# Degrees, h W1 and the order of the attention layer: three rearrangements of a four-layer graph kernel on one core

## The chip, the cores and the metric

The kernel runs on one NeuronCore of a Trainium2 chip. The time is device microseconds (us) of that core. TensorE (PE) multiplies matrices, VectorE (DVE), ScalarE (ACT) and GpSimd (POOL) work on elements, and the DMA queues bring the 4096 x 4096 adjacency matrix from memory again and again. Nearly everything is fp32; behind layer 0 only the targets' terms go through TensorE in bf16.

## The reference

Four graph layers, each added to its input and layer-normalised. N = 4096 nodes, F = 128 features.

```python
x = layernorm(x + L0(x, adj))   # masked attention with two scalars per node (not touched by the change)
x = layernorm(x + L1(x, adj))   # twice: T0 W0 + T1 W1 + T2 W2, T1 = adj T0, T2 = 2 adj T1 - T0, then elu
x = layernorm(x + L2(x, adj))   # 4 heads: tau = adj^T * exp(max(.2 C, C)); z = (adj^T * tau / sum tau) @ h'
x = layernorm(x + L3(x, adj))   # h W_self + (adj h / deg) W_neigh, deg = max(sum of a row of adj, 1)
```

L1 needs four products with adj. L2 needs, for each head, the elementwise tau (summed by a matmul into `den`) and tau * adj (multiplied with the head's features into `num`). L3 needs one product with adj and the row sums `deg`.

## The kernel before

The stages follow each other in time: layer 0 until about 345 us, four products of the Chebyshev layer (345 to 1425 us), the attention layer in eight passes (four column windows `mp` of 1024 targets, two pairs of heads `hp`), of which the first runs beside the fourth product, and the end. The last layer's product runs in "pieces" (one matmul each) between the steps of the attention passes.

The degrees come from DVE additions beside the first product and eight short PE passes per block; h W1 is multiplied after the transposition of the third product's block:

```python
def degree(a, first_one):                       # called for each of the 64 chunks of the first product
    s = l1h.tile([P, 2, IB], F32, name="dhalf")
    nc.vector.tensor_add(s, a[:, 0:2, :], a[:, 2:4, :])
    ...                                         # two more additions of 512 columns into dsum
for ib, blk, p in propagate(lambda jt: x[:, jt, :], finished, degree):
    nc.scalar.copy(t1T[:, blk], p)
    for k in range(TB):
        nc.tensor.matmul(pd[:, k:k + 1], dsum[:, k * P:(k + 1) * P], ones, start=True, stop=True)
    ...
for ib, blk, p in propagate(lambda jt: v[:, jt, :]):        # third product
    ...
    for k in range(TB):
        nc.tensor.matmul(q[:, k, :], lvT[:, k * P:(k + 1) * P], ident, start=True, stop=False)
        for hh in range(HH):
            nc.tensor.matmul(q[:, k, :], hT[:, hh, ...], W1B[:, HH + hh, :], start=False, stop=hh == HH - 1)
```

A pass of the attention, 32 steps of 128 source nodes; the scheduler was free to reorder it:

```python
for nt in range(NT):
    ...                                                     # a: 128 x 1024 of adj; sq = a[:, 0:OWN]^2 by ScalarE
    for h in range(2):
        nc.vector.scalar_tensor_tensor(tau[:, h, :], D[h], E(h), a, op0=ALU.max, op1=ALU.mult)
    nc.vector.scalar_tensor_tensor(tau2[:, 0, 0:OWN], D[0][:, 0:OWN], E(0), sq, op0=ALU.max, op1=ALU.mult)
    nc.gpsimd.tensor_tensor(tau2[:, 0, OWN:WB], tau[:, 0, OWN:WB], a[:, OWN:WB], ALU.mult)
    nc.gpsimd.tensor_tensor(tau2[:, 1, :], tau[:, 1, :], a, ALU.mult)
    product(den, nt, tau, True)                             # four matmuls in four column groups
    late.append((nt, tau2))
    if len(late) > 1:
        product(num, *late.pop(0), False)
    yield                                                   # here one piece of the last layer's product
...                                                         # copies, transposes, z = num / den, all in one lump
```

`D[h]` is the term of the targets of head h, which TensorE writes into PSUM (`d`) at the start of a pass, and `E(h)` that of the sources. `OWN` is 704. After the second pass of a window, `layer3_block` normalises two blocks of 512 nodes and multiplies them with the last weights, also in one lump.

Of the kernel before, what the change touches and what calls it, by code (L numbers as in the profile page):

```python
# [32 lines left out]
def adj_resnorm_d4(ctx: ExitStack, tc: tile.TileContext, x_in, xT_in, adj, adjT, w0g, w0gT, a0, w1a, b1a,  # L33
# [54 lines left out]
    cs = const.tile([P, NT, H], F32, name="cs")  # L88
    flag = const.tile([1, 1], I32, name="flag")
# [19 lines left out]
    def normalize(r, g, on_act=False):  # L109

        tb = slice(g * TB, (g + 1) * TB)
        s = small.tile([P, TB], F32, name="rstd")
        nc.vector.tensor_scalar_add(s, mv[:, tb, 1], LN_EPS)
        nc.scalar.activation(s, s, AF.Sqrt)
        nc.vector.reciprocal(s, s)
        if on_act:
            m = small.tile([P, TB], F32, name="mean")
            nc.vector.scalar_tensor_tensor(m, mv[:, tb, 0], -1.0, s, op0=ALU.mult, op1=ALU.mult)
        for k in range(TB):
            if on_act:  # L120
                nc.scalar.activation(r[:, k, :], r[:, k, :], AF.Identity, bias=m[:, k:k + 1], scale=s[:, k:k + 1])
            else:
                nc.vector.tensor_scalar(r[:, k, :], r[:, k, :], mv[:, g * TB + k, 0:1], s[:, k:k + 1],
                                        op0=ALU.subtract, op1=ALU.mult)
# [322 lines left out]
    def network(usual):  # L447

        with ExitStack() as whole:
# [4 lines left out]
            with ExitStack() as first, ExitStack() as l1h_pool:  # L454
# [6 lines left out]
                if usual:  # L461
                    finished = layer0(ld, ps_acc, ps_tr, ps_mm)
                dv = state.tile([96, N], BF16, name="dv")
# [17 lines left out]
                def propagate(stationary, order=range(NB), look=None):  # L481


                    for ib in range(NB):
                        p = ps_acc.tile([P, IB], F32, name="pacc")
                        for n, c in enumerate(order):
                            a = chunk(ld, adjT, ib, c)
                            if look:
                                look(a, n == 0)
                            for k in range(TB):  # L490
                                nc.tensor.matmul(p, stationary(c * TB + k), a[:, k, :], start=n == 0 and k == 0,  # L491
                                                 stop=n == NB - 1 and k == TB - 1)
                        yield ib, slice(ib * IB, (ib + 1) * IB), p
# [8 lines left out]
                dsum = l1h.tile([P, IB], F32, name="dsum")  # L502

                def degree(a, first_one):

                    s = l1h.tile([P, 2, IB], F32, name="dhalf")
                    nc.vector.tensor_add(s, a[:, 0:2, :], a[:, 2:4, :])
                    if first_one:
                        nc.vector.tensor_add(dsum, s[:, 0, :], s[:, 1, :])
                    else:  # L510
                        nc.vector.tensor_add(dsum, dsum, s[:, 0, :])
                        nc.vector.tensor_add(dsum, dsum, s[:, 1, :])


                for ib, blk, p in propagate(lambda jt: x[:, jt, :], finished, degree):
                    nc.scalar.copy(t1T[:, blk], p)
                    pd = ps_mm.tile([P, TB], F32, name="pmm")
                    for k in range(TB):
                        nc.tensor.matmul(pd[:, k:k + 1], dsum[:, k * P:(k + 1) * P], ones, start=True, stop=True)
                    nc.vector.tensor_scalar_max(rdeg[:, ib * TB:(ib + 1) * TB], pd, 1.0)  # L520
                    q = transpose4(ps_tr, "ptr", lambda k: t1T[:, (ib * TB + k) * P:(ib * TB + k + 1) * P])
                    nc.vector.tensor_copy(t1[:, ib * TB:(ib + 1) * TB, :], q)
                nc.vector.reciprocal(rdeg, rdeg)
# [20 lines left out]
                for ib, blk, p in propagate(lambda jt: v[:, jt, :]):  # L544
                    lvT = l1w.tile([P, IB], F32, name="t2T")
                    nc.scalar.copy(lvT, p)
                    q = ps_tr.tile([P, TB, F], F32, name="ptr")
                    for k in range(TB):
                        nc.tensor.matmul(q[:, k, :], lvT[:, k * P:(k + 1) * P], ident, start=True, stop=False)
                        for hh in range(HH):  # L550
                            nc.tensor.matmul(q[:, k, :], hT[:, hh, (ib * TB + k) * P:(ib * TB + k + 1) * P],  # L551
                                             W1B[:, HH + hh, :], start=False, stop=hh == HH - 1)
# [73 lines left out]
            def attention(l2w, bufs, mp, hp):  # L626


                D = []
                for h in range(2):  # L630
                    d = ps_d.tile([P, 2, IB], F32, name=f"d{h}")
                    for mb in range(2):
                        nc.tensor.matmul(d[:, mb, :], selD[:, 2 * hp + h, :],
                                         dv[:, mp * WB + mb * IB:mp * WB + (mb + 1) * IB], start=True, stop=True)
                    D.append(d.rearrange("p b i -> p (b i)"))
                num = ps_nd.tile([P, IB], F32, name="num")
                den = ps_nd.tile([P, IB], F32, name="den")

                def product(acc, nt, r, is_den):
                    for h in range(2):  # L640
                        for mb in range(2):
                            q = 32 * (2 * h + mb)
                            nc.tensor.matmul(acc[q:q + 32, :], weights(nt, 2 * hp + h, is_den),  # L643
                                             r[:, h, mb * IB:(mb + 1) * IB], start=nt == 0, stop=nt == NT - 1)

                late = []
                for nt in range(NT):
                    if nt % 2 == 0:
                        a2t = ld.tile([P, 2, WB], F32, name="chunk")
                        nc.sync.dma_start(a2t, adj[mp, nt // 2])  # L650
                    a = a2t[:, nt % 2, :]
                    sq = l2w.tile([P, OWN], F32, name="sq", bufs=2)
                    nc.scalar.activation(sq, a[:, 0:OWN], AF.Square)  # L653
                    tau = l2w.tile([P, 2, WB], F32, name="tau", bufs=bufs)
                    tau2 = l2w.tile([P, 2, WB], F32, name="tau2", bufs=bufs)
                    E = lambda h: es[:, nt, 2 * hp + h:2 * hp + h + 1]
                    for h in range(2):
                        nc.vector.scalar_tensor_tensor(tau[:, h, :], D[h], E(h), a, op0=ALU.max, op1=ALU.mult)  # L658
                    nc.vector.scalar_tensor_tensor(tau2[:, 0, 0:OWN], D[0][:, 0:OWN], E(0), sq,  # L659
                                                   op0=ALU.max, op1=ALU.mult)  # L660
                    nc.gpsimd.tensor_tensor(tau2[:, 0, OWN:WB], tau[:, 0, OWN:WB], a[:, OWN:WB], ALU.mult)  # L661
                    nc.gpsimd.tensor_tensor(tau2[:, 1, :], tau[:, 1, :], a, ALU.mult)  # L662
                    product(den, nt, tau, True)
                    late.append((nt, tau2))
                    if len(late) > 1:
                        product(num, *late.pop(0), False)
                    yield
                product(num, *late.pop(0), False)
                nd = l2w.tile([P, 2, IB], F32, name="nd")
                nc.scalar.copy(nd[:, 1, :], den)  # L670
                nc.scalar.copy(nd[:, 0, :], num)
# [145 lines left out]
```

## Time and profile before

| | before |
|---|---|
| time, median of the first three runs | 2348.3 us (2347.94 to 2351.55) |
| profiled span | 2345.0 us |
| start of the fourth product | 1110.2 us |
| fourth product and first pass, until the copy of `den` | 347.1 us |
| seven further passes, from copy of `den` to copy of `den` | 800.4 us |
| from the last copy of `den` to the end | 87.2 us |

The last four rows divide the span of the profile and add up to it: they are taken from the timeline, the first from TensorE's first matmul with `w`, the borders of the passes from ScalarE's copies `nd<-den`. The question in each part is which engine's work sets the distance between two such marks. The views that answer it are shown in the prediction; one more is the list of what VectorE waited for in the seven passes (columns: instruction that waited, what released it, us in total, times, longest):

```profile
DVE tau L658 <- issue: 15.0, 16, 6.4
DVE acc L721 <- PE pp L712: 7.9, 2, 4.0
DVE rd L674 <- PE px L101: 7.6, 7, 3.1
DVE tau L658 <- PE den L643: 4.3, 5, 1.0
DVE tau L659 <- PE num L643: 4.2, 7, 1.0
```

The stages of the finishing of a pass (`rd`) and the additions of finished product blocks (`acc`) are among them, and VectorE ran no attention operation while they waited: in the longest wait of `acc`, 3.97 us until 1836.41 us, the attention operation ahead of it had started at 1831.16 us, the next one started at 1837.02 us.

### The profile page before, as it was taken

How to read it: one execution, taken by the hardware profiler on the slowest of the kernel's cores; microseconds unless marked ns; L12 is line 12 of the kernel's file. 1: busy time of each engine (PE TensorE's matmuls, PEld its weight loads, DVE VectorE, ACT ScalarE, POOL GpSimd, SP SyncE). 2: the span in 40 equal slices, each digit the busy share in tenths (PEclk: the TensorE clock that was granted, in tenths of full speed). 3: DMA queues.
4: the chain of work that ended last, by engine and by line, in shares of the span. 5: the costliest groups of instructions: out<-in, count | busy, mean ns of one | idle time of the engine just before them, and what ended most of it. 6: DMA issues, size and time to landing. Idle time of an engine off the chain costs nothing.

```text
span 2345.0 us, 23138 instructions
## 1 busy us (share of the span) xinstructions
PE 2233.3 (95%) x8742; PEld 851.9 (36%) x8742; DVE 1378.7 (59%) x1991; ACT 480.1 (20%) x708; POOL 847.2 (36%) x541
## 2 busy tenths in 40 slices
PE   5899999999999999999999998889999999999988
PEld 3333454444444444444433332112222222222233
DVE  5454478775011100000167556999799999999965
ACT  6665100000000000000122222232223222322220
POOL 0000000000000000000044334999798899889950
PEclk8899999999999999999999998999999999999999
DMA  9785668888766777777866764446565665566555
GB/s 380 299 318 194 233 204 276 289 292 294 270 233 234 251 251 258 261 256 264 280 242 240 271 239 162 150 153 237 215 234 180 216 232 216 207 224 235 221 187 184
DMA packets 85337, 561.75 MB, mean 240 GB/s; under 512 B 9568, under 2 KB 15712, under 8 KB 17760
## 3 DMA queue, kind: packets, MB, share of 16 engines
q1 hardware_dynamic: 76928, 554.73, 66.5%
q10 hardware_dynamic: 8288, 5.44, 0.7%
q8 instruction: 71, 1.16, 0.2%
q14 instruction: 50, 0.41, 0.1%
HBM read 558.04 MB, written 2.10 MB: 239 GB/s over the span
## 4 chain that ended last, share of the span: by engine, by line
PE 85%; DVE 9%; DMA 3%; issue 2%; ACT 1%; POOL 1%; ACTq 0%; DVEq 0%; POOLq 0%
PE pacc L491 28%; PE pp L712 10%; PE den L643 10%; PE pacc L318 10%; PE pp L747 10%; PE num L643 7%; DVE tau L658 5%; DMA chunk<-in_adjT 2%; PE pmm L532 2%; PE px L101 1%; PE num L712 1%; PE pden L306 1%; DVE tau L659 1%; PE px L698 1%; PE ptr L313 1%
## 5 line engine op out<-in xcount | busy, mean ns | idle before, releaser
L658 DVE SCALAR_TENSOR_TENSOR tau<-d,es,chunk 128x1024 f32<-128x1024 f32 x512 | 634.9, 1277 | 22.4 <-issue 15.0
L662 POOL TENSOR_TENSOR tau<-tau,chunk 128x1024 f32<-128x1024 f32 x256 | 611.1, 2387 | 54.3 <-DVE tau L658 45.7
L643 PE MATMUL den<-tau,cs 128*32 128x512 f32 x2048 | 457.4, 604 | 8.7 <-DVE tau L658 8.2
L621 POOL TENSOR_TENSOR x<-x,B2R 128x512 f32<-128x512 f32 x8 | 10.1, 1266 | 1217.3 <-DMA chunk<-in_adjT 1121.8
L643 PE MATMUL num<-tau,hc 128*32 128x512 f32 x2048 | 414.8, 601 | 31.1 <-POOL tau L662 26.6
L653 ACT ACTIVATE sq<-chunk 128x704 f32<-128x704 f32 x256 | 201.3, 791 | 606.1 <-DVE tau L659 531.4
L661 POOL TENSOR_TENSOR tau<-tau,chunk 128x320 f32<-128x320 f32 x256 | 225.6, 881 | 111.9 <-PE num L643 45.8
L659 DVE SCALAR_TENSOR_TENSOR tau<-d,es,sq 128x704 f32<-128x704 f32 x256 | 241.8, 945 | 17.1 <-PE num L643 14.1
L712 PE MATMUL pp<-chunk,xT 128*128 128x512 f32 x448 | 242.6, 635 | 6.1 <-DMA chunk<-in_adjT 5.1
L747 PE MATMUL pp<-chunk,w 128*128 128x512 f32 x512 | 235.9, 603 | 1.2 <-DVE t2T L753 1.2
L491 PE MATMUL pacc<-chunk,x 128*128 128x512 f32 x512 | 223.6, 594 | 0.0
L491 PE MATMUL pacc<-chunk,t 128*128 128x512 f32 x512 | 223.6, 592 | 0.0
L491 PE MATMUL pacc<-chunk,v 128*128 128x512 f32 x512 | 221.4, 592 | 0.0
L318 PE MATMUL pacc<-chunk,hw 128*128 128x512 f32 x408 | 196.6, 622 | 2.7 <-DVE hw L383 2.7
L643 PEld LDWEIGHTS num<-tau,hc 128*32 128x32 f32 x2048 | 82.1, 109 | 248.7 <-POOL tau L662 83.5
L643 PEld LDWEIGHTS den<-tau,cs 128*32 128x32 f32 x2048 | 85.8, 108 | 223.1 <-issue 102.1
L553 DVE COPY w<-ptr 128x512 f32<-128x512 f32 x8 | 5.5, 692 | 246.1 <-PE ptr L551 246.1
L491 PEld LDWEIGHTS pacc<-chunk,v 128*128 128x128 f32 x512 | 97.1, 190 | 121.5 <-issue 121.5
L491 PEld LDWEIGHTS pacc<-chunk,t 128*128 128x128 f32 x512 | 96.1, 190 | 114.8 <-issue 114.8
L747 PEld LDWEIGHTS pp<-chunk,w 128*128 128x128 f32 x512 | 92.3, 190 | 124.7 <-issue 117.8
L491 PEld LDWEIGHTS pacc<-chunk,x 128*128 128x128 f32 x512 | 95.8, 190 | 113.4 <-issue 113.4
L712 PEld LDWEIGHTS pp<-chunk,xT 128*128 128x128 f32 x448 | 70.4, 189 | 168.5 <-issue 145.7
(180 smaller groups left out, 1542.1 us busy)
## 6 DMA issues: line engine op xcount, KB each, us to landing
chunk<-in_adjT SPq DMA_DIRECT2D x386, 1024.0 KB, 4.8
chunk<-in_adj SPq DMA_DIRECT2D x128, 1024.0 KB, 4.8
keep<-in_adjT SPq DMA_DIRECT2D x13, 1024.0 KB, 4.8
xT<-in_xT ACTq DMA_DIRECT2D x8, 256.0 KB, 5.8
out<-o ACTq DMA_DIRECT2D x8, 256.0 KB, 3.7
W1A<-in_w1a ACTq DMA_DIRECT2D x1, 384.0 KB, 6.5
W1B<-in_w1b ACTq DMA_DIRECT2D x1, 384.0 KB, 7.3
W0T<-in_w0gT ACTq DMA_DIRECT2D x1, 64.0 KB, 5.9
```

The source lines that it names most:

```text
L101: nc.tensor.transpose(p[:, k, :], src(k), ident)
L318: nc.tensor.matmul(p, hw[:, j * TB + k, :], a[:, k, :], start=first and k == 0, stop=last and k == TB - 1)
L491: nc.tensor.matmul(p, stationary(c * TB + k), a[:, k, :], start=n == 0 and k == 0, stop=n == NB - 1 and k == TB - 1)
L532: nc.tensor.matmul(ph, W1A[:, k, hh * P:(hh + 1) * P], r, start=k == 0, stop=k == 2)
L643: nc.tensor.matmul(acc[q:q + 32, :], weights(nt, 2 * hp + h, is_den), r[:, h, mb * IB:(mb + 1) * IB], start=nt == 0, stop=nt == NT - 1)
L653: nc.scalar.activation(sq, a[:, 0:OWN], AF.Square)
L658: nc.vector.scalar_tensor_tensor(tau[:, h, :], D[h], E(h), a, op0=ALU.max, op1=ALU.mult)
L659: nc.vector.scalar_tensor_tensor(tau2[:, 0, 0:OWN], D[0][:, 0:OWN], E(0), sq, op0=ALU.max, op1=ALU.mult)
L661: nc.gpsimd.tensor_tensor(tau2[:, 0, OWN:WB], tau[:, 0, OWN:WB], a[:, OWN:WB], ALU.mult)
L662: nc.gpsimd.tensor_tensor(tau2[:, 1, :], tau[:, 1, :], a, ALU.mult)
L712: nc.tensor.matmul(p, y[:, (2 * mp + c) * TB + k, :], a[:, k, :], start=c == 0 and k == 0, stop=c == 1 and k == TB - 1)
L747: nc.tensor.matmul(p, w[:, c * TB + k, :], a[:, k, :], start=c == 0 and k == 0, stop=c == NB - 1 and k == TB - 1)
```

## The change

The intent: (1) ScalarE sums the rows of adj in the second pass of each window, where the chunk is in SBUF anyway, so that the first product loses its ones-passes; (2) h W1 is added into the PSUM bank of the third product by two wide matmuls; (3) the seven passes are put in program order on PE, DVE, ACT and POOL, with the finishing stages strewn over the steps, den one step and num two steps behind, and pieces handed out by a credit that grows by 1.3 a step; what is left of the pieces goes between the stages of the last chain.

```diff
-                for ib, blk, p in propagate(lambda jt: x[:, jt, :], finished, degree):
+                for ib, blk, p in propagate(lambda jt: x[:, jt, :], finished):
                     nc.scalar.copy(t1T[:, blk], p)
-                    for k in range(TB):
-                        nc.tensor.matmul(pd[:, k:k + 1], dsum[:, k * P:(k + 1) * P], ones, start=True, stop=True)
...
+                def times_w1(p, ib):
+                    for hh in range(HH):
+                        nc.tensor.matmul(p, W1B[:, HH + hh, :], hT[:, hh, ib * IB:(ib + 1) * IB], start=False, stop=False)
-                for ib, blk, p in propagate(lambda jt: v[:, jt, :]):
+                for ib, blk, p in propagate(lambda jt: v[:, jt, :], beside=times_w1):
...
+                    nc.scalar.activation(sq, a[:, 0:OWN], AF.Square)
+                    if self.hp == 1:
+                        junk = l2w.tile([P, WB], BF16, name="junk")
+                        nc.scalar.activation(junk, a, AF.Copy, accum_out=deg[:, nt, self.mp:self.mp + 1])
...                                             (a step: tau 0, then the square part of 0, then tau 1)
+                    nc.vector.scalar_tensor_tensor(tau[:, 0, :], D[0], E(nt, 0), a, op0=ALU.max, op1=ALU.mult)
+                    nc.gpsimd.tensor_tensor(tau2[:, 0, OWN:WB], tau[:, 0, OWN:WB], a[:, OWN:WB], ALU.mult)
+                    nc.vector.scalar_tensor_tensor(tau2[:, 0, 0:OWN], D[0][:, 0:OWN], E(nt, 0), sq, ...)
+                    nc.vector.scalar_tensor_tensor(tau[:, 1, :], D[1], E(nt, 1), a, op0=ALU.max, op1=ALU.mult)
+                    nc.gpsimd.tensor_tensor(tau2[:, 1, :], tau[:, 1, :], a, ALU.mult)
...
+            with tc.manual_schedule(engines={PE, DVE, Activation, Pool}):
+                for s, (mp, hp, nt) in enumerate(steps):
+                    ...
+                    tau, tau2 = heads.step(nt, l2w, (3, 4), a, sq)
+                    ahead = ...squares(...)             # of the next step
+                    ...                                 # den of the step before, num of the one before that
+                    while credit >= 1.0:
+                        credit -= 1.0
+                        if one(pieces):
+                            credit = 0.0
+                    one(chains)                         # one stage of finish() or layer3_blocks()
+                for chain in (before[0].finish(), layer3_blocks(NW - 1)):
+                    for _ in chain:
+                        one(pieces)                     # left-over pieces between the last chain's stages
```

A step is a function that all eight passes use; the program order covers the last seven.

## The prediction

> **What bounds the kernel now.** I read the page first: one engine row says PE 95% busy[...]. So I asked for the busy time of every engine in windows cut at the pass boundaries (taken from the chain and the timeline), then for the timeline inside one step, then for what VectorE (DVE) waited for.
>
> The page's groups give the four elementwise operations of a step:
>
> ```profile
> L658 DVE SCALAR_TENSOR_TENSOR tau<-d,es,chunk 128x1024 f32<-128x1024 f32 x512 | 634.9, 1277 | 22.4 <-issue 15.0
> L662 POOL TENSOR_TENSOR tau<-tau,chunk 128x1024 f32<-128x1024 f32 x256 | 611.1, 2387 | 54.3 <-DVE tau L658 45.7
> L661 POOL TENSOR_TENSOR tau<-tau,chunk 128x320 f32<-128x320 f32 x256 | 225.6, 881 | 111.9 <-PE num L643 45.8
> L659 DVE SCALAR_TENSOR_TENSOR tau<-d,es,sq 128x704 f32<-128x704 f32 x256 | 241.8, 945 | 17.1 <-PE num L643 14.1
> ```
>
> Two of 1.28 us and one of 0.945 us are 3.50 us of DVE per step. In the timeline of an undisturbed step they overlap by some 0.08 us each:
>
> ```profile
> 1503.04 0.94 DVE L659 SCALAR_TENSOR_TENSOR tau<-d,es,sq 128x704 f32<-128x704 f32 x1
> 1503.90 2.47 DVE L658 SCALAR_TENSOR_TENSOR tau<-d,es,chunk 128x1024 f32<-128x1024 f32 x2
> 1506.28 0.94 DVE L659 SCALAR_TENSOR_TENSOR tau<-d,es,sq 128x704 f32<-128x704 f32 x1
> ```
>
> The step repeats every 3.24 us with no hole on DVE; GpSimd (0.87 + 2.37 us) fills the same 3.24 us, so the two are balanced and DVE, which has all the small work besides, is the bound. The windows show how far each pass is from it (columns: window, its length, then busy us of PE, weight loads, DVE, ACT, GpSimd, then clock and DMA; the first seven rows are the passes, the last two the end):
>
> ```profile
> 1457.00:1566.50 109.50, 90.50 (x528) 17.58 (x526) 104.69 (x98) 27.55 (x37) 104.66 (x67) 1.00 0.45 154
> 1566.50:1691.60 125.10, 118.70 (x630) 31.46 (x634) 108.68 (x121) 36.28 (x61) 103.85 (x67) 1.00 0.60 219
> 1691.60:1797.70 106.10, 99.44 (x574) 24.98 (x566) 104.75 (x98) 28.04 (x39) 103.20 (x66) 1.00 0.62 218
> 1797.70:1917.60 119.90, 115.19 (x612) 31.46 (x612) 111.71 (x124) 33.21 (x56) 103.89 (x67) 0.99 0.58 209
> 1917.60:2028.00 110.40, 107.88 (x588) 27.13 (x588) 107.54 (x102) 26.42 (x36) 104.19 (x67) 1.00 0.62 229
> 2028.00:2148.00 120.00, 115.38 (x612) 31.58 (x613) 111.78 (x125) 33.31 (x56) 104.02 (x67) 0.99 0.58 210
> 2148.00:2257.40 109.40, 107.07 (x586) 26.99 (x586) 106.91 (x102) 24.96 (x32) 103.16 (x67) 1.00 0.61 227
> 2257.40:2279.40 22.00, 15.38 (x51) 8.05 (x50) 5.15 (x27) 7.79 (x21) 1.56 (x1) 0.77 0.22 77
> 2279.40:2345.00 65.60, 56.25 (x152) 25.01 (x150) 35.27 (x152) 2.28 (x10) 0.00 (x0) 0.95 0.56 193
> ```
>
> The seven passes last 800.4 us; DVE is busy 104.69+108.68+104.75+111.71+107.54+111.78+106.91 = 756.1 us of it. So 44 us is all that a better order can win there, most of it in passes 2, 4 and 6 (16.4, 8.2, 8.2 us), which carry the normalisation and weight products of the last layer ("layer-3 blocks") in one lump. The worst hole, where DVE starts again only after 6.4 us:
>
> ```profile
> 1684.25 0.94 DVE L659 SCALAR_TENSOR_TENSOR tau<-d,es,sq 128x704 f32<-128x704 f32 x1
> 1691.57 1.28 DVE L658 SCALAR_TENSOR_TENSOR tau<-d,es,chunk 128x1024 f32<-128x1024 f32 x1 [6.37 <-issue]
> ```
>
> From 350 us on the big products of the Chebyshev layer (the "second layer" of the title) are bound by PE: in 350 to 606 us PE is busy 255.0 of 256 us at clock 1.00, DVE 169.5.
>
> [...] The degree additions here took exactly 1224 ns; the attention operation, with one PSUM operand, takes 1277 ns. [...] eight weight passes in four column groups (an fp32 matmul shows as two passes of 0.43 us) took 1.06 us and sixteen 1.90 us, and between a full-array piece and the next tiled group there are 1.06 us where its two passes alone are 0.86:
>
> ```profile
> 1425.40 1.06 PE L643 MATMUL den<-tau,cs 128*32 128x512 f32 x8
> 1426.28 1.90 PE L643 MATMUL num<-tau,hc 128*32 128x512 f32 x16
> ...
> 2101.22 1.12 PE L712 MATMUL pp<-chunk,xT 128*128 128x512 f32 x2
> 2102.28 1.05 PE L643 MATMUL den<-tau,cs 128*32 128x512 f32 x4
> ```
>
> **Part by part.**
>
> (1) Degrees leave the first product. DVE loses 64 x 1.22 + 112 x 0.69 + 8 x 0.68 = 161 us, all beside PE, worth nothing there. PE loses eight ones-passes per block, which stand alone between matmuls from 433.62 to 434.43 us: 0.81 x 8 = 6.5 us, on the path. ACT gains 128 sums over 1024 columns. Between the square of 704 columns (791 ns) and the 2048-column sum (1912 ns) the slope is 0.83 ns a column, so about 1.06 us and 0.19 us to read the sum: 1.25 + 0.79 = 2.0 us of ACT per 3.24 us step in the second pass of each column window. Hidden.
>
> (2) h W1 into the product's PSUM. Now 24 short passes (identity and W1, 128 columns each) run from 946.42 to 949.21 us: 2.79 us per block. After: two 512-column matmuls, 4 x 0.43 = 1.72 us, and four transposes, 0.44 us as elsewhere: 2.16. Gain 0.63 x 8 = 5.0 us, on the path.
>
> (3) The seven passes. In the order of the built kernels the matmuls of a step go to PE in whole groups: 137 groups of exactly 8 tiled matmuls between mode changes after, 22 before (52 of six, 48 of four, 40 of two), and 338 changes against 402. A step with one piece then needs on PE 1.72 + 0.1 + 1.06 = 2.9 us, with two 3.8, with none 1.8; eight steps of a block (6, 1 and 1 of them) 23.0 us, against DVE's 8 x 3.24 + 0.62 = 26.6. So DVE stays the bound. PE runs one to two steps behind DVE, the chain stages are split so that DVE meets finished operands, and reading d1 last lets d0 be refilled during it. DVE's work falls by two additions that move to the end (1.2 us). I allow 6 us for what is left: half a microsecond per pass for d, and eight statistics pairs in dependent order, about 0.15 us more each in three windows. Passes: 756 - 1 + 6 = 761, gain 39 us.
>
> (4) The end. Pieces start 18 steps into a window instead of at once, and still take 64 steps: counting the built order, 176 of 192 are done at the end of the last pass, so 16 of 0.86 us (13.8 us) fall into it. Before, DVE's last step ended at 2257.4, the final product began in earnest at 2279.4 with four matmuls (3.4 us) already done: 18.6 us. After, from DVE's end: the last group waits for GpSimd's 2.4 us multiplication (3.6 us), reciprocal and z about 7.7, because an addition of a left-over block stands ahead of them, addition and statistics 11.5, scale 12.3, eight normalisations of 0.41 on ACT 15.8, then four rounds of weight product and two copies, about 2.1 us, with two transposes and copies of 1.2 us: 24.8; four pieces are left, 3.4 us: 28.2. Twelve pieces are hidden. Cost 28.2 - 18.6 = about 9.5 us; the 65 us of final product stay.
>
> (5) The weights' DMAs move earlier in the built order, and DVE waits for them inside layer 0. Before, DVE waited 1.75 us there. I take it as nothing, plus or minus 2.
>
> Sum: 2348.3 - 6.5 - 5.0 - 39 + 9.5 = 2307; ACT's early squares and a PE that is no longer idle (clock 0.77 at the end) may give a little: **2305 us**, 1.8% faster.
>
> **Rivals.** (a) PE becomes the bound in steps with pieces: if groups of four ran one after the other, a step would need 8 x 0.43 + 1.06 = 4.5 us, over 192 steps +240 us, about 2540. The 1.06 and 1.90 us above speak against it; what speaks for a mild form is that PE is at 87% of the step and any lumps (transposes, weight products of 0.86 us) come on top: +10 to +15 us, 2320. (b) The strict order makes DVE wait for ACT, on which squares now queue behind copies that wait for PE, or for a chunk: six buffers hold 12 steps of attention alone, 8 with pieces. Squares stand a whole step ahead, and a chunk lives about 4 steps of its 8. If it fails, half of the gain goes: 2325. (c) All 44 us are won and the left-over pieces hide in the end's holes[...]: 39 becomes 43, 9.5 becomes 4: 2296, over 2% faster. (d) The removed DVE additions count: no, PE was busy 255 of 256 us.
>
> **Range.** The two large terms, 39 (30 to 44) and 9.5 (4 to 13), decide. 2% is 2301.3 us, four under my figure, and needs nearly (c). Range 2290 to 2322; faster by over 2% 0.33, within 2% 0.65, slower 0.02.
>
> **What would show it.** Blocks of the first product 28.0 instead of 28.8 us apart, of the third 31.4 instead of 32.0; passes of 105 to 112 us with DVE busy all but 1 us of each, PE with waits for DVE; from DVE's last attention step to the final product some 28 us. Wrong, if DVE in a pass waits for PE's den or num or for sq, if the step with a piece is over 3.35 us, or if GpSimd shows no idle time while DVE does.

That the change leaves the three operations as long as they were was the author's assumption; the profile after has them at 1276, 945 and 1278 ns (1277, 945 and 1277 before). 2348.3 - 6.5 - 5.0 - 39 + 9.5 comes to 2306.8 us, and the step from there to 2305 us is an allowance without a measured size.

The seven passes of 32 steps lie in 1457 to 2257 us of the profile of before. Two of the estimates can be set beside the traces: sixteen tiled passes (1.72 + 0.1 us in the prediction) took 1.85 us in the profile after, from 1368.85 us to the next full-array matmul at 1370.70, and a pair of statistics instructions followed the one before it after 0.26 us in the profile of before (2263.68 and 2263.94 us) and after 0.39 us in that of the changed kernel (1802.01 and 1802.40 us). To the clock at the end: TensorE of the kernel before was busy 0.10 us of 2261.4 to 2265.8 us and was granted 0.50 of its clock in 2265.8 to 2273.0 us.

## The result, and the profile after

| | before | after | difference |
|---|---|---|---|
| time, median of four runs | 2349.93 us (2347.94 to 2351.89) | 2315.15 us (2313.34 to 2318.32) | -34.8 us |
| profiled span | 2345.0 | 2316.5 | -28.5 |
| start of the fourth product | 1110.2 | 1100.7 | -9.5 |
| fourth product and first pass | 347.1 | 354.7 | +7.6 |
| seven passes | 800.4 | 764.0 | -36.4 |
| end | 87.2 | 97.1 | +9.9 |

The ratio is 0.9853, 95% interval 0.9836 to 0.9871: 1.5% faster, within the 2%. A ratio here is always the mean time of one kernel's runs over that of the other's runs of the same rounds, so it is not quite the ratio of the medians quoted. The profiled run of before (2347.03 us) was faster than its four timed ones and that of after (2318.32 us) was its slowest, which is why the spans differ less than the medians.

The windows of the changed kernel, cut at its pass borders (columns as in the prediction; the first row starts with the first attention operation of the second pass, the last two are the end):

```profile
1454.40:1562.20 107.80, 76.59 (x508) 17.79 (x508) 104.63 (x99) 60.68 (x100) 101.32 (x65) 0.98 0.46 156
1562.20:1673.10 110.90, 99.54 (x580) 28.76 (x580) 110.55 (x117) 36.14 (x59) 103.93 (x67) 0.98 0.51 180
1673.10:1777.90 104.80, 102.05 (x589) 30.33 (x588) 104.50 (x98) 59.05 (x98) 103.73 (x67) 1.00 0.68 242
1777.90:1890.20 112.30, 107.62 (x613) 31.68 (x612) 111.36 (x118) 35.58 (x60) 104.04 (x67) 0.98 0.63 225
1890.20:1997.40 107.20, 104.44 (x589) 29.96 (x588) 106.90 (x102) 57.25 (x94) 103.97 (x67) 1.00 0.65 236
1997.40:2110.50 113.10, 106.68 (x613) 31.75 (x612) 112.46 (x121) 34.16 (x57) 103.98 (x67) 1.00 0.62 223
2110.50:2217.70 107.20, 104.44 (x591) 29.85 (x593) 106.89 (x104) 55.67 (x92) 103.91 (x67) 1.00 0.66 236
2217.70:2252.00 34.30, 32.21 (x104) 14.97 (x97) 9.89 (x30) 8.21 (x21) 2.43 (x2) 0.95 0.56 191
2252.00:2316.50 64.50, 53.39 (x146) 23.80 (x144) 35.26 (x152) 1.65 (x8) 0.00 (x0) 0.93 0.57 194
```

In six of the seven passes VectorE's busy time is within 1 us of the length of the pass. The three passes that carried lumps before (125.1, 119.9 and 120.0 us) are now 110.9, 112.3 and 113.1 us. ScalarE is busy 55 to 61 us instead of 25 to 28 where it sums.

What VectorE still waits for in the passes is three kinds of waits where before there were nine (the costliest five were shown above), and two of the three are at the border of the first two passes:

```profile
DVE tau L644 <- ACT sq L621: 3.5, 2, 3.2
DVE tau L642 <- PE d L632: 3.4, 1, 3.4
DVE tau L642 <- POOL tau L643: 1.5, 5, 0.3
```

The operations themselves are as long as before, and now TensorE stands idle in front of `den` for 63.0 us, 55.4 of them for VectorE (8.7 and 8.2 us on the page of before; groups: count, busy us, mean ns, idle us in front and what ended most of it):

```profile
L659 PE MATMUL den<-tau,cs 128*32 128x512 f32 x2048 | 392.9, 608 | 63.0 <-DVE tau L646 55.4
...
L642 DVE SCALAR_TENSOR_TENSOR tau<-d,es,chunk 128x1024 f32<-128x1024 f32 x256 | 326.6, 1276 | 7.4 <-PE d L632 4.1
L646 DVE SCALAR_TENSOR_TENSOR tau<-d,es,chunk 128x1024 f32<-128x1024 f32 x256 | 327.1, 1278 | 0.1
```

So the passes went as planned. The surprise is in the stage that the prediction did not work out: the fourth product with the first pass got 7.6 us longer. The timeline of TensorE in one block of that product shows how (start, length, instruction, count of passes):

```profile
1352.13 1.04 PE L659 MATMUL den<-tau,cs 128*32 128x512 f32 x2
1353.11 1.10 PE L591 MATMUL px<-xT,WD 128*96 128x512 f32 x2
1354.14 1.04 PE L659 MATMUL den<-tau,cs 128*32 128x512 f32 x2
1355.11 1.13 PE L777 MATMUL pp<-chunk,w 128*128 128x512 f32 x2
1356.17 1.05 PE L659 MATMUL den<-tau,cs 128*32 128x512 f32 x4
1357.15 2.84 PE L777 MATMUL pp<-chunk,w 128*128 128x512 f32 x6
```

A step's eight `den` passes fall into groups of 2, 2 and 4, with full-array matmuls between them. Each small group takes as long as a whole one: groups of 2, 4, 6 and 8 tiled passes between full-array matmuls took 1.04, 1.05, 1.06 and 1.07 us in this block. In the kernel before, which had 2 and 6 here, the blocks are 40.95 us apart at the end of the stage; in the changed kernel they are 42.1. The experiment below with the old order shows the same place. The 7.6 us themselves carry noise: the fifth block of the product took from 41.95 to 45.79 us in the nine profiles with the old order there, and 45.79 is the one of before, at a granted clock of 0.96. The whole stage took 342.9 to 347.1 us in those nine, and 354.6 to 354.7 in the four profiles with the new order and 704 columns.

### The profile page after: what moved, and what is told of

Its sections match the earlier page's. It is cut to its first block, busy times and chain, and to the rows that moved or that the text cites. A ratio compares the mean times of both kernels' runs of the same rounds, so it can differ in the third digit from the quotient of the medians. Undisturbed runs are those within 1.5% of the kernel's fastest.

```text
span 2316.5 us, 22706 instructions
## 1 busy us (share of the span) xinstructions
PE 2189.3 (95%) x8550; PEld 848.2 (37%) x8550; DVE 1235.3 (53%) x1789; ACT 609.3 (26%) x960; POOL 846.3 (37%) x541
## 5 line engine op out<-in xcount | busy, mean ns | idle before, releaser
L659 PE MATMUL den<-tau,cs 128*32 128x512 f32 x2048 | 392.9, 608 | 63.0 <-DVE tau L646 55.4
L659 PE MATMUL num<-tau,hc 128*32 128x512 f32 x2048 | 374.0, 599 | 4.7 <-POOL tau L647 4.0
L642 DVE SCALAR_TENSOR_TENSOR tau<-d,es,chunk 128x1024 f32<-128x1024 f32 x256 | 326.6, 1276 | 7.4 <-PE d L632 4.1
L646 DVE SCALAR_TENSOR_TENSOR tau<-d,es,chunk 128x1024 f32<-128x1024 f32 x256 | 327.1, 1278 | 0.1
L731 PE MATMUL pp<-chunk,xT 128*128 128x512 f32 x448 | 236.5, 630 | 0.0
L659 PEld LDWEIGHTS den<-tau,cs 128*32 128x32 f32 x2048 | 64.0, 107 | 306.5 <-DVE tau L646 169.8
L659 PEld LDWEIGHTS num<-tau,hc 128*32 128x32 f32 x2048 | 91.3, 110 | 155.0 <-issue 138.3
```

The costliest lines, as they stand in the source:

```text
L642: nc.vector.scalar_tensor_tensor(tau[:, 0, :], D[0], E(nt, 0), a, op0=ALU.max, op1=ALU.mult)
L646: nc.vector.scalar_tensor_tensor(tau[:, 1, :], D[1], E(nt, 1), a, op0=ALU.max, op1=ALU.mult)
L659: nc.tensor.matmul(acc[q:q + 32, :], weights(nt, 2 * self.hp + h, is_den), r[:, h, mb * IB:(mb + 1) * IB], start=nt == 0, stop=nt == NT - 1)
L731: nc.tensor.matmul(p, y[:, (2 * mp + c) * TB + k, :], a[:, k, :], start=c == 0 and k == 0, stop=c == 1 and k == TB - 1)
```

## The experiments

Twelve kernels ran, all correct. The runs of before beside them had medians of 2347.89 to 2350.72 us. Where an experiment is built on another, the text says so. The same marks divide all profiles:

| run | time | ratio to before (95%) | start of 4th product | with 1st pass | seven passes | end |
|---|---|---|---|---|---|---|
| w1_only | 2343.98 | 0.9979 (0.9966 to 0.9993) | 1105.4 | 343.1 | 802.3 | 87.5 |
| w1_and_degrees | 2347.89 | 0.9996 (0.9982 to 1.001) | 1099.4 | 345.2 | 817.2 | 87.1 |
| no_program_order | 2380.46 | 1.0128 (1.0112 to 1.0143) | 1099.2 | 354.7 | 832.1 | 91.4 |
| stages_in_one_lump | 2352.89 | 1.0012 (0.9997 to 1.0028) | 1098.9 | 354.7 | 810.8 | 89.5 |
| sums_in_all_passes | 2315.64 | 0.9851 (0.9836 to 0.9866) | 1099.7 | 354.7 | 763.9 | 95.9 |
| own736 | 2319.77 | 0.9872 (0.9857 to 0.9887) | 1101.3 | 352.2 | 771.1 | 96.2 |
| first_pass_old_order | 2306.78 | 0.9819 (0.9805 to 0.9832) | 1101.2 | 345.5 | 764.6 | 95.5 |
| no_left_overs | 2304.20 | 0.9809 (0.9795 to 0.9822) | 1098.7 | 343.9 | 766.7 | 91.1 |
| early_targets | 2305.66 | 0.9814 (0.9800 to 0.9827) | 1100.0 | 345.5 | 766.1 | 93.3 |
| own688 | 2299.43 | 0.9790 (0.9776 to 0.9803) | 1096.9 | 342.9 | 764.3 | 91.1 |
| short_tail | 2302.53 | 0.9803 (0.9789 to 0.9818) | 1097.8 | 345.5 | 767.5 | 90.3 |
| kept_warm | 2296.00 | 0.9769 (0.9756 to 0.9783) | 1097.9 | 343.0 | 763.0 | 90.3 |

The column of the fourth product's start also shows the noise of one profile: the other eleven kernels do the same work until there as the changed one, whatever comes later, and range from 1096.9 to 1101.3 us, about the size of the smaller effects. Such effects are read from the marks nearest to them.

### w1_only: the kernel before with h W1 in PSUM

```diff
-                        nc.tensor.matmul(q[:, k, :], lvT[:, k * P:(k + 1) * P], ident, start=True, stop=False)
-                        for hh in range(HH):
-                            nc.tensor.matmul(q[:, k, :], hT[...], W1B[:, HH + hh, :], start=False, stop=hh == HH - 1)
+                    q = transpose4(ps_tr, "ptr", lambda k: lvT[:, k * P:(k + 1) * P])
+                            (two matmuls of 512 columns into the product's bank, as in the change)
```

> The kernel before with h W1 alone moved into the product's PSUM. My theory (24 short passes of 2.79 us leave each of the eight blocks of the third product, 1.72 us of wide matmuls and 0.44 us of transposes come in): blocks 31.4 instead of 32.0 us apart, 5.0 us in all, and the kernel 5 us faster than before. Rival: the eight copies that end the blocks were waited for anyway and the gain is swallowed by the next product's start: 0 us.

Measured: blocks of the third product 31.43 us apart (32.00 before), and the ratio 0.9979 is 4.9 us of 2348, with an interval of 1.6 to 8.0 us. The theory holds, the rival's 0 us lies outside the interval.

### w1_and_degrees: both changes of the second layer in the old third layer

```diff
-    (degree(), dsum and the ones-passes of the first product)
                     nc.scalar.activation(sq, a[:, 0:OWN], AF.Square)
+                    if hp == 1:
+                        junk = l2w.tile([P, WB], BF16, name="junk", bufs=1)
+                        nc.scalar.activation(junk, a, AF.Copy, accum_out=deg[:, nt, mp:mp + 1])
```

> The kernel before with both changes of the second layer (h W1 in PSUM, degrees by ScalarE in the second pass of each window), but the old order of the third layer. My theory: 11.5 us faster than before (5.0 + 6.5), if ScalarE's 1.25 us per step stays hidden beside the old order too. Rival 1: ScalarE's sums delay copies that the layer-3 blocks wait for, so that passes with sums get longer and less than 8 us is left. Rival 2: the 1.7 us that the weights' earlier loads seem to have cost layer 0 appear here too, where their place in the program is the old one except for the removed additions: then 9 to 10 us.

Measured: 0.9 us faster than before, not 11.5. The product did its part: its blocks are 27.94 instead of 28.80 us apart, and the fourth product starts 10.8 us earlier than before. But the seven passes take 817.2 us, 14.9 us more than in w1_only, and 12 us of that are in the last three (116.0, 123.0 and 113.7 us instead of 110.4, 119.9 and 110.4). What VectorE waited for in these three passes, here:

```profile
DVE rd L663 <- PE px L102: 9.0, 3, 4.3
DVE tau L648 <- ACT sq L639: 6.0, 5, 2.3
```

and in w1_only:

```profile
DVE rd L676 <- PE px L101: 2.5, 3, 0.9
```

There was no wait for `sq` there at all. The longest of the waits for `sq` shows how a sum gets in the way (columns of a timeline, in brackets the idle time before and what ended it):

```profile
1964.31 2.47 DVE L647 SCALAR_TENSOR_TENSOR tau<-d,es,chunk 128x1024 f32<-128x1024 f32 x2
...
1966.04 1.06 ACT L642 ACTIVATE junk<-chunk 128x1024 bf16<-128x1024 f32 x1 [7.06 <-DMA chunk<-in_adj]
...
1968.28 0.77 ACT L639 ACTIVATE sq<-chunk 128x704 f32<-128x704 f32 x1
...
1969.09 0.95 DVE L648 SCALAR_TENSOR_TENSOR tau<-d,es,sq 128x704 f32<-128x704 f32 x1 [2.31 <-ACT sq L639]
```

At 1964.31 us VectorE is already reading this step's chunk, so the chunk that the square needs has arrived. But ScalarE runs two sums of the next chunk ahead of the square (the second starts at 1967.22 us), and it has waited 7.06 us for that transfer. In these three passes ScalarE waited 65.3 us for chunks in front of sums. The longest wait for the transposes looks alike: at 2148.83 us they had waited 3.15 us for the copy of `den`, which stood behind four sums and two squares; the first of these sums had waited 5.96 us for its chunk. In these two waits it is the place of the sums in ScalarE's order that costs, those 7.06 and 5.96 us, more than the sums' own 1.23 us each (1043 and 188 ns in the profile after). How much of the whole loss comes this way was not tested by itself. Rival 1 was right: in the old order the sums are not hidden. Rival 2's size cannot be told from the noise of that column.

The 14.9 us compare two profiles, one of them the slowest run of its kernel. By the medians w1_and_degrees is 3.9 us slower than w1_only, although its fourth product starts 6.0 us earlier; that leaves some 10 us for the sums, an estimate.

### sums_in_all_passes: the changed kernel with nearly twice the sums

```diff
+                    if self.hp == 0 and self.mp > 0:
+                        junk = l2w.tile([P, WB], BF16, name="junk")
+                        nc.scalar.activation(junk, a, AF.Copy, accum_out=spare[:, nt:nt + 1])
```

> The changed kernel with ScalarE's sum of 1024 columns in the first passes of the windows too (three of the four more, its result unused). Theory: in program order the sums are hidden (ScalarE 57 to 61 of 107 us busy where it sums), so twice the sums cost nothing: 2315 us within 3. Rival: the sums delay squares and copies in those passes too, as they seem to do in the old order, where 128 sums went with some 17 us of longer passes: then 96 more sums cost 8 to 13 us.

Measured: 2315.64 us, the passes 763.9 us against 764.0. In the new order 96 more sums cost nothing. That the first 128 cost nothing either was not run by itself; it follows from VectorE, which is busy all but 0.3 us of each pass with sums after the first. In the changed kernel each sum stands behind the square of its own chunk, and the profile shows 0.0 us of idle time before the 128 sums. The work that cost 10 to 15 us in the old order is free in the new one.

### no_program_order: the changed kernel, order left to the scheduler

```diff
-            with tc.manual_schedule(engines={PE, DVE, Activation, Pool}):
+            if True:
```

> The changed kernel, with the stages strewn as there, but the third layer's order on the engines left to the scheduler instead of taken from the program. Theory: the program order is what puts PE's tiled matmuls into whole groups and keeps VectorE's queue free of operations that wait; without it the seven passes lose again 15 to 35 us (780 to 795 us instead of 764), the kernel 2330 to 2350 us. Rival: strewing the stages alone does it, and the scheduler would have kept them so: 2315 us within 5.

Measured: 2380.46 us, slower than before, the passes 832.1 us. That is outside what I expected, on the far side of the theory. VectorE's two largest waits in its passes:

```profile
DVE tau L642 <- issue: 32.3, 14, 7.0
DVE tau L642 <- PE den L659: 32.1, 26, 2.0
```

The second is a wait for TensorE's den in front of a write of tau; I read it as a tau buffer that TensorE has not finished with. The same wait had cost 4.3 us in the kernel before, as shown above. So the strewn stages need the fixed order: left to the scheduler, they made the passes longer than the lumps had.

### stages_in_one_lump: program order kept, stages not strewn

```diff
-                    one(chains)
+                    while chains:
+                        one(chains)
```

> The changed kernel with program order kept, but all stages of a finishing pass and of the layer-3 blocks run in one lump in the step where they become ready, as the kernel before had them. Theory: program order and strewing work only together, because in a fixed order VectorE's next attention operation stands behind each stage that waits for PE or ScalarE. Seven finishes with some 3 us of waits each and three pairs of layer-3 blocks with 10 to 16 us: the passes take 800 to 830 us instead of 764, the kernel 2350 to 2380 us. Rival: program order alone gives the gain (PE's whole groups), strewing is only a nicety: 2320 to 2330 us.

Measured: 2352.89 us, the passes 810.8 us, as the theory said; the rival falls. The wait is not where I had put it (I had thought of VectorE's own chain stages), but in what ScalarE runs:

```profile
DVE tau L644 <- ACT sq L621: 43.0, 4, 13.5
DVE z L676 <- PE px L103: 6.1, 7, 1.3
```

The next square comes behind a lump of copies, of which the four to `xT` in the lump shown here waited 2.16 or 2.17 us each for TensorE's weight product. ScalarE's timeline of this lump ends so:

```profile
1822.95 0.37 ACT L717 COPY xT<-px 128x256 f32<-128x256 f32 x1 [2.17 <-PE px L715]
1823.22 0.38 ACT L718 COPY x<-px 128x256 f32<-128x256 f32 x1
1823.48 2.84 ACT L621 ACTIVATE sq<-chunk 128x704 f32<-128x704 f32 x4
```

Four squares follow in 2.84 us with no wait between them. VectorE's longest wait for a square was 13.5 us in this run; the square itself takes 0.79 us.

The four corners of part 3 are then: old order and lumps with the sums 817.2 us; strewn without program order 832.1; program order without strewing 810.8; both 764.0. (The first corner differs from the others also in the order within a step and in buffers.) Neither half is worth more than 6.4 us alone, and one of them loses 14.9.

### own736 and own688: the balance between VectorE and GpSimd

```diff
-OWN = 704
+OWN = 736     (own736, on the changed kernel)      or      688     (own688, on no_left_overs)
```

> The changed kernel with VectorE squaring 736 instead of 704 columns of the first target. If VectorE bounds the passes (busy all but 6 us of 764): 32 columns are 33 ns a step, 1.07 us a pass, so the seven passes take 7.5 us longer, 2322 us. If GpSimd bounds them (busy 726 of 764, 3.27 us a step): its step gets 75 ns shorter, and the passes stay or get up to 10 us shorter: 2305 to 2315 us. If PE bounds them: nothing changes, 2315 us.

Measured: passes 771.1 us, 7.1 longer, 1.0 us each. That is what VectorE's extra columns cost: its operation takes 945 ns for 704 columns and 1277 for 1024, so 32 columns are 33 ns, and 32 steps of them 1.06 us. The whole kernel lost only 4.6 us in the medians, because in the profile the stage with the first pass was 2.5 us shorter and the end 0.9 us.

> The run without left-overs with VectorE squaring 688 instead of 704 columns. At 736 columns the seven passes took 7.1 us longer, 1.0 us each. If that slope goes on downwards: 16 columns are 0.5 us a pass, 3.5 us in all, 2300.7 us. GpSimd's step grows by 37 ns to 3.28 us, 104.9 us a pass, which is above only the shortest pass (104.8 us); so I expect 3 us, 2301 us. Rival: GpSimd has no slack in plain steps (both fill 3.24 us), and each pass gets 1 us longer instead: 2309 us or more.

Measured: passes 764.3 instead of 766.7 us, 0.3 to 0.5 us less in each of the last six, and 2299.43 us (no_left_overs 2304.20). The theory holds in the passes, where it gives 2.4 of the 4.8 us. In the profiles the rest lies ahead of the passes: 1.8 us before the fourth product, where the two kernels do the same work, and 1.0 us in the stage with the first pass. Both are of the size of the noise.

### first_pass_old_order: the step's old order in the first pass alone

```diff
                     nc.vector.scalar_tensor_tensor(tau[:, 0, :], D[0], E(nt, 0), a, op0=ALU.max, op1=ALU.mult)
+                    if old: (tau 1 here, then the square part of 0, then GpSimd's part of 0)
...
-                        tau, tau2 = heads.step(nt, l2a, (2, 2), *heads.squares(nt, l2a, 2))
+                        tau, tau2 = heads.step(nt, l2a, (2, 2), *heads.squares(nt, l2a, 2), old=True)
```

> The changed kernel, with the old order of a step's three VectorE operations (target 0, target 1, square part of 0) in the first attention pass alone, which runs beside the last Chebyshev product. Theory: the new order is what made that product's blocks 42.1 instead of 40.95 us, because the tiled matmuls come in other groups between the full-array ones; then the blocks return to 41 us and the kernel gets 4 to 6 us faster than the changed kernel (2309 to 2311 us). Rival: the blocks got longer for another reason (the pools' or scheduler's placement after the weights' buffer moved), then they stay at 42.1 and the time at 2315 within 2 us.

Measured: 2306.78 us, 8.4 us below the changed kernel, more than I expected. The blocks are 40.95 us apart again, and TensorE's timeline at the place shown above:

```profile
1349.31 1.04 PE L665 MATMUL den<-tau,cs 128*32 128x512 f32 x2
1350.28 1.10 PE L591 MATMUL px<-xT,WD 128*96 128x512 f32 x2
1351.31 1.06 PE L665 MATMUL den<-tau,cs 128*32 128x512 f32 x6
1352.30 3.70 PE L783 MATMUL pp<-chunk,w 128*128 128x512 f32 x8
```

The last two lines are followed by the next tiled group at 1355.93 us, so they take 1355.93 - 1351.31 = 4.62 us. In the changed kernel the same fourteen passes, the last four lines shown above, were followed by the next group at 1359.92 us and took 1359.92 - 1354.14 = 5.78 us, because two passes of the product stand in the middle of the group. That is the 1.16 us per block. The product as a whole (from its start to its last matmul) is 5.6 us shorter than in the changed kernel, 313.6 instead of 319.2. Another 3.6 us are won at the border behind it: from the product's end to the copy of `den` it takes 31.88 us here, 31.87 before, and 35.44 in the changed kernel, where TensorE finishes the first pass later. So the new order costs 9.2 us in this stage of the profile.

### no_left_overs: no pieces for the end

On first_pass_old_order:

```diff
-                                chains.append(start_product(b.mp, 1.3))
+                                chains.append(start_product(b.mp, 2.0 if b.mp == NW - 2 else 1.3))
```

> The changed kernel with the old order in the first pass (2306.8 us alone), and the pieces of the last interleaved product issued at up to two a step instead of 1.3, so that none of the 192 is left for the end: 40 pieces in each of the last two passes instead of 32. Theory: PE has room for eight more pieces of 0.86 us a pass, the passes keep 113 and 107 us, and in the end the four pieces after the chain, and some delay of the chain by pieces ahead of its transposes, fall away: 3.5 to 5 us faster, 2302 to 2303 us. Rival: with two pieces PE needs 3.8 us in a step of 3.24 us, VectorE waits for buffers, and the two passes lengthen by as much or more: 2306 to 2312 us.

Measured: the end is 4.4 us shorter (91.1 instead of 95.5), as the theory has it, but the sixth of the seven passes is 2.9 us longer (116.0 instead of 113.1), as the rival has it. The time is 2.6 us lower in the medians, and the intervals of the two overlap. The last pass, with 40 pieces as well, stayed at 107.3 us.

### early_targets: the border of the first two passes

On no_left_overs:

```diff
                         yield
+                    follow = Heads(0, 1)
+                    follow.targets()
+                    first_squares.append((follow, follow.squares(0, l2f, 1)))
                     heads.product(False, *late)
```

(`z` and `xb` share memory with that first square and `junk`, to make room.)

> The run without left-overs, with the next pass's targets and first square issued ahead of the first pass's last weight product, which waits for GpSimd. Theory: VectorE's 3.3 us of waiting at the border of the first two passes come from the targets standing on TensorE behind that product; with them ahead, VectorE goes on 2 us earlier, and as VectorE bounds what follows, the kernel is 2 us faster, 2302 us. Rival: TensorE is still behind with the first pass's products there, and the targets come no earlier: 0 us.

Measured: no gain in time (2305.66 us). VectorE's wait did shrink, from 3.27 us (in no_left_overs and in first_pass_old_order) to 1.91:

```profile
1447.10 1.28 DVE L642 SCALAR_TENSOR_TENSOR tau<-d,es,chunk 128x1024 f32<-128x1024 f32 x1 [1.91 <-PE d L632]
```

The second pass became 0.5 us shorter (107.8 us), and the rest went into differences elsewhere that are as large as the noise; what the shared memory costs was not tested by itself. The theory was right about the wait and its 2 us too large; in the time nothing shows.

### short_tail: a shorter chain at the end

On no_left_overs:

```diff
+                        if mp == NW - 1 and j == 1:
+                            nc.vector.tensor_scalar(r, r, s[:, k:k + 1], m[:, k:k + 1], op0=ALU.mult, op1=ALU.add)
...
+                        if mp == NW - 1:
+                            nc.vector.tensor_copy(x[:, two, :], q[:, :, 1, :])
...
+                for n, _ in enumerate(layer3_blocks(NW - 1)):
+                    if 6 <= n < 10:
+                        next(final[(n - 6) // 2])
+                        next(final[(n - 6) // 2])
```

> The run without left-overs (2304.2 us), with a shorter serial chain after the last attention step: the second block normalised by VectorE instead of queueing on ScalarE ahead of the first block's copy (1.4 us), one of the two copies of each weight product on VectorE (0.4 us a round, four rounds), and eight instead of four pieces of the final product, from two output blocks, put into TensorE's holes between the rounds (3 us). Theory: the end is a chain of short operations with TensorE idle between them, so these add up to 4 to 5 us: 2299 to 2300 us. Rival: TensorE is what the end waits for from the first weight product on, because its matmuls run slower after the idle time (1.63 and 2.07 us instead of 0.66 and 1.13 there): less than 2 us.

Measured: the end 90.3 us against 91.1, the time 2302.53 us, within the interval of no_left_overs. The rival holds. The windows of no_left_overs, the kernel that it builds on, show what happens after the last transposes of the pass (columns as above; the eighth number of a row is the granted clock):

```profile
2213.00:2219.50 6.50, 0.30 (x3) 0.06 (x1) 4.88 (x22) 0.74 (x3) 0.00 (x0) 0.76 0.26 110
2219.50:2222.70 3.20, 1.64 (x5) 0.73 (x5) 0.00 (x0) 3.15 (x8) 0.00 (x0) 0.50 0.00 0
2222.70:2228.60 5.90, 5.44 (x12) 2.96 (x12) 0.00 (x0) 1.30 (x4) 0.00 (x0) 0.67 0.00 0
```

TensorE is busy 0.30 of 6.50 us while VectorE takes the statistics, and then is granted 0.50 of its clock for 3.2 us and 0.67 on average in the 5.9 us after that. In first_pass_old_order, where left-over pieces keep it busy for 6.23 of 6.40 us, the granted clock stayed at 1.00:

```profile
2214.80:2221.20 6.40, 6.23 (x17) 2.54 (x14) 5.03 (x23) 0.70 (x3) 0.00 (x0) 1.00 0.59 223
2221.20:2224.40 3.20, 1.31 (x4) 0.55 (x4) 0.56 (x1) 3.16 (x9) 0.00 (x0) 1.00 0.90 289
2224.40:2230.00 5.60, 5.58 (x20) 3.25 (x21) 0.00 (x0) 1.88 (x5) 0.00 (x0) 1.00 0.15 60
```

So the left-over pieces were perhaps not pure loss: with them the granted clock was 1.00 in these windows, without them 0.50 and 0.67. That the idle time is the cause is my reading of these profiles.

### kept_warm: all together, with matmuls of no use in the gap

short_tail, early_targets and 688 columns, and:

```diff
+                spare = ps_d.tile([P, 2, IB], F32, name="d0")
+                for n in range(6):
+                    nc.tensor.matmul(spare[:, n % 2, :], ident, xT[:, 0:IB], start=True, stop=True)
```

> The runs with 688 columns, early targets and the short tail together, and in addition six matmuls of no use (0.86 us each, into the free target buffer) on TensorE while the end's chain is on VectorE. In the profile of the short tail TensorE stood idle 6.2 us there and its granted clock then was 0.50 in the next 6.8 us, with the first weight product's two matmuls taking 2.07 us instead of 1.13; with left-over pieces the clock stayed at 1.00. Theory: the idle time is what ate the short tail's gain; with TensorE kept busy the clock stays 1.00, and from VectorE's last attention step to the last instruction it takes 82 to 83 us instead of 86.9; the kernel takes 2294 to 2295 us (2299.4 with 688 columns alone, 1 us less by early targets, 4 us less at the end). Rival: the clock falls for another reason (no chunk transfer ran there either), or TensorE's order costs the gain: 86 us or more at the end and 2298 us.

Measured: 2296.00 us, the fastest kernel, 2.3% below before. But the end is 90.3 us, exactly as in short_tail, so the useless matmuls gave nothing that shows; counted as in the expectation, from VectorE's last attention operation to the issue of the last output's transfer, it is 87.0 us against 86.9. The windows show the clock that was granted:

```profile
2207.60:2213.00 5.40, 5.38 (x15) 2.16 (x12) 4.52 (x20) 0.21 (x1) 0.00 (x0) 1.00 0.31 129
2213.00:2216.00 3.00, 1.31 (x4) 0.55 (x4) 1.49 (x6) 2.07 (x5) 0.00 (x0) 0.96 0.00 0
2216.00:2222.30 6.30, 5.62 (x8) 2.67 (x9) 0.42 (x1) 0.54 (x2) 0.00 (x0) 0.50 0.00 0
```

The clock stayed at 1.00 through the six matmuls and fell all the same 3 us after them, when TensorE had been busy for 1.31 of 3.0 us; first_pass_old_order had 1.31 of 3.2 us and kept its clock. What decides between these two is open; ahead of it TensorE had been busy 8.67 of 10.40 us in kept_warm and 11.41 of 11.60 us in first_pass_old_order. The experiment therefore does not show what a full clock would be worth there. Compared with own688 the gain is 1.3 us in the passes (107.2 instead of 108.6 us in the second, from the early targets) and 0.8 us at the end; the medians differ by 3.4 us and the intervals of the ratios overlap.

## Why the prediction was right or wrong

The range (2290 to 2322) held; the time was 10 us too low.

**Part 1, the degrees.** Right on TensorE: 0.86 us a block for 0.81 predicted. ScalarE's sum took 1043 ns and 188 ns for the reading, against 1.06 and 0.19 us. The word "hidden" was right of the changed kernel (sums_in_all_passes) and wrong of the old order, where the sums cost 10 to 15 us. So the parts of the sum were not independent: by itself, part 1 is worth nothing (w1_and_degrees against w1_only), and part 3 is worth correspondingly more, about 53 us from 817.2 to 764.0 us. That the prediction's 6.5 and 39 add up nearly right is because both were taken for the kernel with all parts.

**Part 2, h W1.** Right: 31.43 us a block for 31.4, and 4.9 us of the time for 5.0.

**Part 3, the seven passes.** Right in mechanism, 2.6 us off in size: 36.4 us instead of 39. In the windows shown, 763.3 us together, VectorE was busy 757.3 us (755 expected) and lost 6.0 us (6 expected), of which 3.2 are one wait for a square at the border of the first two passes, a kind of wait that the prediction had listed as a sign of being wrong; another 3.4 us of waiting for the targets lie just ahead of the first window. It is VectorE's work that sets the passes: 32 columns more made them 7.1 us longer (own736), 16 fewer 2.4 us shorter (own688). The order does it together with the strewing, neither alone.

**Part 4, the end.** From VectorE's last attention step to the final product's last addition it took 87.1 us instead of 77.7: 9.4 for the 9.5 predicted. From that addition to the end the changed kernel took 1.7 us more (11.7 instead of 10.0 us), a distance that ranged from 10.0 to 12.7 us over the runs. The final product began 27.6 us after VectorE's last attention step, at 2245.31 us (28.2 predicted). The last block's chain was done after 25.0 us instead of 24.8, and there luck helped: the terms written for it do not add up to 24.8 (15.8 + 4 x 2.1 + 2 x 1.2 is 26.6), while the normalisation was done 1.5 us earlier than predicted, after 14.3 us. Nor was the mechanism quite the one given. The prediction counted four pieces as left after the chain and the others as hidden at no cost. Without left-overs the end is 4.4 us shorter, which is about the 3.4 us of those four and a little delay; but TensorE, idle there, was then granted 0.50 and 0.67 of its clock (no_left_overs). The changed kernel itself was granted 0.56 and 0.58 in 2232 to 2236 us, where first_pass_old_order, with the same end, kept 1.00 and took 85.7 us from the last attention step to the last addition instead of 87.1.

**Part 5, the weights' loads.** Nothing to be seen: the first block of the first product ended at 377.9 us against 376.2, but in other runs with the same second layer at 374.1 to 378.4.

**What the sum left out.** The sum reads "2348.3 - 6.5 - 5.0 - 39 + 9.5 = 2307". It has no term for the fourth product and the first pass, which the change touches through the new order of a step. The prediction's count of mode changes, "338 changes against 402", is that of the seven passes; it shows none for this stage. Counted in the traces, from the first copy of `den` to the end there are 332 changes against 398, but in the stage with the fourth product 100 against 92, and 91 in first_pass_old_order. The missing term is 7.6 us in the profiles of before and after, and 9.2 us against the same kernel with the old order there. The remark that "ACT's early squares and a PE that is no longer idle" may give a little went the wrong way as well.

**The rivals.** (a) TensorE as the bound: not at 32 pieces a pass; with 40, one of two passes lengthened by 2.9 us. (b) VectorE waiting for ScalarE: once, 3.2 us, at the first border. It was nearer than I thought: it is what happened when the stages were not strewn (43.0 us). (c) The left-overs hidden: no, 4.4 us of the end hang on them. (d) The removed DVE additions: no gain of their own.

## What to carry to other kernels

Work put on an engine with idle time was hidden here only where the engine's order let the urgent work past: the same sums cost 10 to 15 us in one order and nothing in the other, where in the longest waits a sum whose chunk had not arrived stood ahead of a square whose chunk had. And fixed order with lumps or strewn stages without fixed order were worth little or less than nothing, together 53 us. When a change reorders a helper that several stages share, work out each stage in which it runs, above all one where another engine is the bound: here a better order for VectorE-bound steps cost 9.2 us beside a TensorE-bound product. Behind a gap with left-over pieces TensorE's granted clock was 1.00 in first_pass_old_order and 0.56 in the changed kernel, behind the gap without them 0.50 (no_left_overs), with the six matmuls of kept_warm 0.50 as well; so read the granted clock after the gap before counting on the time saved.
